# Scan stage of a Mamba block: moving kept output-projection pieces away from the softplus and gate blocks, and adding state pairs by DMA in eight more steps

## The chip, the cores and the metric

The kernel runs on one core of one Trainium2 chip. The metric is the time of one execution on the device, in microseconds (us). The core has four engines that compute, each with its own queue, worked off strictly in order: TensorE (PE: matmuls), VectorE (DVE), ScalarE (ACT: activation functions) and GpSimd (POOL). SyncE (SP) only issues DMA transfers. Engines wait for each other through semaphores.

## The reference, cut to what matters

The whole model is two layers, each a graph or state-space block and a mixture of experts, on 4096 tokens of width 256. The change touches only the state-space (Mamba) block of layer 0:

```
h = relu(adj @ layernorm(x) @ gcn_w + gcn_b);  h = layernorm(h) * ln_g + ln_b
xc, z = split(h @ w_in)                       # 512 channels each
u = silu(causal_conv4(xc) + conv_b)
dt, B, C = split(u @ w_xp);  dt = softplus(dt @ w_dt + b_dt)
for each token:  state = exp(dt * A) * state + dt * B * u     # 512 channels x 16 states
                 ys = sum over the 16 states of state * C
y = (ys + u * D_skip) * silu(z)
x1 = x + y @ w_out
```

`x1` is then layer-normalised and goes to the first mixture of experts.

## The kernel before

Tokens are worked in NC = 8 chunks of CW = 512. The 512 channels are MB = 4 blocks of 128 partitions. The scan stage is a loop over `n`, `c, i = divmod(n, STEPS)`: chunk c, and STEPS = 32 steps i in a chunk. One step works on one channel block (`m`) and two of the 16 states: `half, g, mi` come from i, so i = 0 to 15 are blocks 0 and 1 (alternating), i = 16 to 31 blocks 2 and 3; g is the pair of states.

The order of the work on TensorE, VectorE, ScalarE and GpSimd is the order in which the Python code issues it (`tc.manual_schedule`). SyncE is not in that list: the order of its DMA issues is chosen by the framework. In one turn of the loop, for step n, the code issues:

- GpSimd: `nxt.inputs` (L1138), the product du x bb for step n+1 into `db` (two buffers); and for mi = 0 SyncE loads bb and cb, rows of B and C spread over all partitions (L1134, 512 KB each, two buffers). Then `steps[n-1].pair()` (L1175): in a paired step a DMA issued by GpSimd adds the second state's half of `hc` to the first.
- VectorE: two scans (L1161), each 128 x 512, which need `da`; after each, ScalarE's `nxt.decay` (L1154) writes one of the next step's two `da` tiles, exp(dt x A), into PSUM. Then pieces of the next chunk's preparation on VectorE (`Front.EARLY`), in the last chunk also pieces of the norm (`NORMS`: L965, a pow on GpSimd L968, L974).
- `cur.product`: ScalarE copies the last state (L1167), VectorE multiplies by cb into `hc` (L1171; six buffers).
- `gate` (L1197) for a block that is complete: VectorE multiplies psy by silu(z).
- `total` (L1183, L1188): TensorE adds `hc` to psy of its channel block (`ps_y`, two banks) by products with the identity, one for a paired step and two for an unpaired one; the first of a block also brings u x D_skip (`dD`), and needs the bank that a gate sets free. A paired step's total comes four turns later, an unpaired one's two turns later.
- A piece of the next chunk's preparation, `Front.PLAN`, or, for i < 8, of this chunk's (keys 32 + i): "xz" are matmuls (L787), "in" copies of ScalarE out of PSUM (L794, L800), "silu 2" (keys 39, so i = 7) an activation on 128 x 2048 (L811). Keys 25 to 28 are softplus: "abs", "exp", "plus", "log" on ScalarE (L850 to L863); "soft" 0 to 3 at i = 28 to 31 are eight products on VectorE (L869 to L877).
- `Tail.step(tails)`: one piece of the output projection (below).
- In the last chunk, norm pieces (`NPIECES`, from i = 8: load of x1, normalise L985, turn L998, logits L1010, keep L1016).
- Pieces of the adjacency product two chunks ahead (not in the last two chunks).

Output projections. In chunks 0 to 5 the finished y is kept in DRAM (`keep_gated`), and its projection by w_out is put off. From step (6,8) the kept projections are worked as `Tail`s, half a chunk each, twelve in a row, t0 to t11 here; those of chunk 6 follow from (7,5). A Tail has three pieces, `product(0)`, `product(1)` and `put`; those of chunks 0 to 2 have an empty piece ahead of `put`. `product` (L929 four products, L933 adds the row of x by an identity product) writes the PSUM tile `ps_out`, of which there is one. `put` (L938) has ScalarE copy it to `xr` with row sums and SyncE store it (L943). The squares of a Tail (L948, L952, ScalarE) are left in `Tail.rest` and issued at the start of the next `Tail.step`. When a Tail starts, the following one's loads (`fetch`: x rows into `xr`, L916, two buffers; kept y, L921, three buffers) are issued.

```
while Tail.rest:
    Tail.rest.pop()()
if tails:
    tails[0].todo.pop(0)()
    if len(tails) > 1 and tails[1].xr is None:
        tails[1].fetch()
```

Before the change `Tail.step` is called once in every turn, so that t4 starts at (6,24), t5 at (6,28), t6 at (7,0), t7 at (7,3), t8 at (7,6) and t9 at (7,9). Steps are paired in chunks 0 to 6, and unpaired in chunk 7.

Of the kernel before, what the change touches and what calls it, by code (L numbers as in the profile page):

```python
# [30 lines left out]
def kernel(ctx: ExitStack, tc: tile.TileContext, out: bass.AP, **a):  # L31
# [5 lines left out]
    NC = N // CW  # L37
# [125 lines left out]
    class Dispatch:  # L163
# [4 lines left out]
        def __init__(self, pool, E, name, batches, c0=0):  # L168

            self.E, self.pool, self.name, self.T, self.c0 = E, pool, name, batches, c0  # L170
            self.t0 = [sum(batches[:b]) for b in range(len(batches))]
            self.NT = NT = sum(batches)
            self.K = 2 * NT * P // TR + E - 1
            self.wv = pool.tile([P, NT, 2], F32, name=f"{name}_wv")
            self.hi = pool.tile([P, 2 * NT], F32, name=f"{name}_hi")
            self.lo = None
            self.row = {}
            self.xd = dram.tile([NT * P, D], F32, name=f"{name}_xd")

            self.S = 1 << (NT // TPC - 1).bit_length()  # L180
            self.ys = dram.tile([2 * self.S * CW + self.K * TR, D], F32, name=f"{name}_ys")
            self.count = pool.tile([P, 1, E], F32, name=f"{name}_count")
            self.start()
            self.sent = []

            self.oh = []
            for T in sorted(set(batches), reverse=True):
                n = batches.count(T)
                t = pool.tile([P, n, 2 * T + 1, E], BF16, name=f"{name}_oh{T}")
                nc.gpsimd.memset(t[:, :, :1, :], 0.0)  # L190
                self.oh += [t[:, b] for b in range(n)]

            self.rev = pool.tile([P, max(batches), E], F32, name=f"{name}_rev")
            nc.vector.tensor_scalar(
                self.rev, iota[:, :E].unsqueeze(1).to_broadcast([P, max(batches), E]),
                -1.0, float(E), ALU.mult, ALU.add,
            )

            self.group = pool.tile([P, NT, 2], BF16, name=f"{name}_group")
            for i in range(2):  # L200
                nc.vector.tensor_scalar(
                    self.group[:, :, i], iota[:, :NT], float(i * self.S * TPC), None, ALU.add
                )
# [385 lines left out]
    with ExitStack() as s1:  # L589
# [56 lines left out]
        STEPS = H * 2 * GS  # L646
# [12 lines left out]
        def propagation(c):  # L659


            halves = psts[c] = []
            for r0 in range(c * CW, c * CW + CW, HW):
                pt = ps_pt.tile([P, DB, HW], F32, name="pt", tag="pt")
                for j4 in range(NT // 4):
                    at = ats.pop(0) if ats else adjacency(r0, j4)
                    for jj in range(4):
                        j = 4 * j4 + jj
                        for k in range(DB):

                            nc.tensor.matmul(  # L671
                                pt[:, k, :], xl[:, j, k * P:(k + 1) * P], at[:, jj, :],
                                start=(j == 0 and k == 0), stop=(j == NT - 1 and k == DB - 1),
                            )
                        yield
                pts = w1p.tile([P, DB, HW], F32, name="pts", bufs=2)
                nc.scalar.copy(pts, pt)
                halves.append(pts)
                yield True
# [203 lines left out]
        def keep_gated(c):  # L883

            yd = dram.tile([P, MB, CW], F32, name=f"yd{c}")
            nc.sync.dma_start(yd, fronts[c].us)
            return yd
# [130 lines left out]


        SLOW = 3  # L1020
        NORMS, NPIECES = {}, {}
        for i, c0, c1 in ((1, 0, 3), (13, 3, 5), (19, 5, 6), (25, 6, 7)):
            NORMS[i] = lambda s0=c0 * TPC, n=(c1 - c0) * TPC: Norm.root(s0, n)
# [90 lines left out]
        class Step:  # L1114
# [3 lines left out]
            def __init__(self, c, i):  # L1118
                self.c, self.i = c, i
                self.half, r = divmod(i, 2 * GS)  # L1120
                self.g, self.mi = divmod(r, 2)
                self.m = 2 * self.half + self.mi
                self.f = fronts[c]


                self.paired = c < NC - 1

            def inputs(self, prev):

# [69 lines left out]
        with tc.manual_schedule(engines={  # L1199
# [13 lines left out]
            for _ in range(2 * NT + 2 - sum(FILLED.values())):  # L1213
                i = min(range(STEPS), key=lambda i: pe[i] - PE_RATIO * dve[i])
# [4 lines left out]
            def advance(k=1, wait=False):  # L1219


                while k > 0:
                    k -= 1
                    if next(prop, None) and wait:
                        break
                return k
# [47 lines left out]
            steps, tails, kept, gated, summed, owed = [], [], {}, [], 0, 0  # L1274
            for n in range(NC * STEPS):
                c, i = divmod(n, STEPS)
                if n == 0:
                    cur = Step(0, 0)
                    cur.inputs(None)
                    das = [cur.decay(0), cur.decay(1)]  # L1280
                steps.append(cur)
                if i == 5 and c > 0:
                    if c < NC - 1:
                        kept[c - 1] = keep_gated(c - 1)
                    else:
                        tails.extend(Tail(c - 1, hh) for hh in range(2))
                if i == 8 and c == NC - 2:
                    tails.extend(
                        Tail(k, hh, kept[k], k < SLOW) for k in range(c) for hh in range(2)
                    )  # L1290
                if i == 8:
                    fr = Front(c + 1) if c + 1 < NC else None
                    prop = propagation(c + 2) if c + 2 < NC else iter(())
                if i == STEPS - 1 and fr is not None:
                    fr.at(i, Front.EARLY)
                nxt = Step(*divmod(n + 1, STEPS)) if n + 1 < NC * STEPS else None
                if nxt is not None:
                    nxt.inputs(cur)
                if n > 0:
                    steps[n - 1].pair()  # L1300
                old, das = das, []
                for j in range(2):
                    cur.scan(j, old[j])
                    if nxt is not None:
                        das.append(nxt.decay(j))
                if 7 < i < STEPS - 1 and fr is not None:
                    fr.at(i, Front.EARLY)
                if c == NC - 1 and i in NORMS:
                    NORMS[i]()
                cur.product()  # L1310
                for k in gated:
                    steps[k].gate()
                gated = []
                while summed < n - 1 and (summed < n - 3 or not steps[summed].paired):
                    steps[summed].total()
                    gated.append(summed)
                    summed += 1
                if i < 8:
                    fronts[c].at(STEPS + i)
                elif fr is not None:  # L1320
                    fr.at(i)
                Tail.step(tails)
                if c == NC - 1:
                    for piece in NPIECES.get(i, ()):
                        piece()
                    if i == 22:
                        last = Last()
                        last.first(1)
                    elif i == 24:
                        last.fetch()  # L1330
                    elif i == 25:
                        last.first(0)
                    elif i in (27, 28):
                        last.residual(i - 27)
                owed = advance(pieces[i] + owed, True)
                if i == 7:
                    while owed:
                        owed = advance(owed, True)
                cur = nxt
# [455 lines left out]
```

## Time and profile before

| | us |
|---|---|
| median of 3 runs | 2412.82 (2411.54 to 2413.08) |
| the profiled execution | 2412.49 |
| its span in the profile | 2410.7 |
| TensorE busy in the span | 2239.3 (93%) |
| VectorE busy | 1648.1 (68%) |
| ScalarE busy | 1194.8 (50%) |
| GpSimd busy | 1144.8 (47%) |
| last scan of the scan stage ends | 1245.5 |

In the lines of the profile that follow, a line of the order of time has: start, length (us), engine, line of the kernel, operation, output<-inputs with partitions x elements, count, and in brackets the time that the engine stood idle before it and what ended that. A line of the list of waits has: who waited and for whom, total us, times, longest. A line of the table of stretches has: the stretch and its length, then busy us (and instructions) of PE, PEld (weight loads), DVE, ACT and POOL, then TensorE's granted clock, the DMA engines' busy share and GB/s.

### The profile page before, as it was taken

The page shows a single profiled execution, that of the slowest core. Times are in us where ns is not written, and L with a number is a line of the kernel's source. Part 1 is how long each engine was busy: PE and PEld are TensorE (multiplying, and loading weights), DVE is VectorE, ACT ScalarE, POOL GpSimd, SP SyncE. Part 2 cuts the span into 40 slices and gives each one's busy share as a digit, 9 for nine tenths or more (in the row PEclk, how much of TensorE's full clock was granted, in tenths as well). Part 3 has the DMA queues.
Part 4 walks back from the last instruction along what each step waited for, and adds up shares of the span by engine and source line. Part 5 has one row for each costly group of instructions (what it writes and reads, how often), then busy time and mean ns, then how long its engine had stood idle before and what let it go on. Part 6 is the DMA issues. An engine that isn't in the chain of part 4 may idle for free. (4 is left out here: it accounts for less than half of the span.)

```text
span 2410.7 us, 28097 instructions
## 1 busy us (share of the span) xinstructions
PE 2239.3 (93%) x9018; PEld 1624.2 (67%) x9018; DVE 1648.1 (68%) x2455; ACT 1194.8 (50%) x2050; POOL 1144.8 (47%) x828
## 2 busy tenths in 40 slices
PE   8999999999999999896997999799999999999985
PEld 7665665656465665553666888667888888877774
DVE  2069999999999999998986411291666667742233
ACT  4255666574655666574753322145555555532321
POOL 1057777777877787775644555310000000045652
PEclk9999999999999999998997999999999999999998
DMA  7279999999999999996848877551444444456786
GB/s 237 83 228 227 241 275 238 274 243 268 247 260 258 238 274 238 271 269 174 270 136 266 295 231 228 162 166 53 143 146 148 146 145 146 148 170 209 230 274 235
DMA packets 293071, 511.58 MB, mean 212 GB/s; under 512 B 25376, under 2 KB 159648, under 8 KB 292016
## 3 DMA queue, kind: packets, MB, share of 16 engines
q1 hardware_dynamic: 246640, 412.64, 54.5%
q0 software_dynamic: 46272, 97.03, 18.7%
q8 instruction: 75, 1.23, 0.2%
q14 instruction: 84, 0.69, 0.1%
HBM read 406.03 MB, written 44.83 MB: 187 GB/s over the span
## 5 line engine op out<-in xcount | busy, mean ns | idle before, releaser
L1138 POOL TENSOR_TENSOR db<-du,bb 128x1024 f32<-128x1024 f32 x256 | 607.1, 2372 | 329.5 <-DVE hc L1171 83.1
L1161 DVE TENSOR_TENSOR_SCAN db<-da,state,db 128x512 f32<-128x512 f32 x512 | 627.2, 1266 | 31.5 <-ACT da L1154 29.3
L671 PE MATMUL pt<-at,gn 128*128 128x256 f32 x2048 | 479.4, 387 | 14.9 <-ACT gn L87 9.2
L671 PEld LDWEIGHTS pt<-at,gn 128*128 128x128 f32 x2048 | 397.1, 195 | 135.7 <-issue 63.1
L1154 ACT ACTIVATE da<-dt,negA 128x512 f32<-128x512 f32 x512 | 346.4, 688 | 249.5 <-DVE db L1161 238.7
L1516 PE MATMUL pf<-gn,f 128*128 128x256 f32 x2048 | 452.0, 380 | 0.0
L1516 PEld LDWEIGHTS pf<-gn,f 128*128 128x128 f32 x2048 | 386.6, 190 | 57.2 <-issue 6.4
L1171 DVE TENSOR_TENSOR hc<-db,cb 128x1024 f32<-128x1024 f32 x256 | 328.0, 1281 | 18.2 <-issue 0.4
L1188 PE MATMUL psy<-hc,ident 128*128 128x512 f32 x576 | 301.6, 618 | 4.6 <-DMA hc<-hc 3.7
L81 POOL TENSOR_TENSOR ln_rs<-ln_rs,mhalf 128x4 f32<-128x4 f32 (+1 forms) x25 | 33.4, 1335 | 507.6 <-DVE ln_rs L80 507.1
L508 DVE TENSOR_TENSOR yk<-ps_y,bk 128x512 f32<-128x512 f32 x73 | 50.4, 691 | 308.9 <-PE ps_y L503 232.2
L1505 ACT ACTIVATE f<-f 128x1024 f32<-128x1024 f32 x128 | 134.6, 1057 | 198.7 <-DVE f L1504 128.2
L518 PE MATMUL ps_h<-xkT,wk 128*128 128x256 f32 x864 | 213.6, 388 | 14.7 <-DVE xkT L543 6.9
L503 PE MATMUL ps_y<-wk,hk 128*128 128x256 f32 x864 | 213.3, 382 | 9.2 <-ACT hk L522 6.6
L1175 POOL DMA_DIRECT2D hc<-hc x224 | 195.0, 870 | 0.2
L518 PEld LDWEIGHTS ps_h<-xkT,wk 128*128 128x128 f32 x864 | 159.1, 192 | 50.6 <-ACT hk L522 11.3
L1504 DVE TENSOR_SCALAR f<-at 128x1024 f32<-128x1024 f32 x128 | 88.1, 688 | 148.0 <-PE pf L1516 134.4
L503 PEld LDWEIGHTS ps_y<-wk,hk 128*128 128x128 f32 x864 | 161.9, 191 | 32.7 <-ACT hk L522 8.4
L1188 PEld LDWEIGHTS psy<-hc,ident 128*128 128x128 f32 x576 | 109.3, 196 | 90.2 <-issue 64.0
L1511 DVE SCALAR_TENSOR_TENSOR cnt<-at,cnt 128x1024 bf16<-128x1024 f32 x120 | 145.9, 1216 | 15.9 <-DMA at<-in_adjT_dram 12.3
L1506 ACT ACTIVATE f<-f 128x1024 f32<-128x1024 f32 x128 | 134.5, 1055 | 3.4
L787 PE MATMUL ps_xz<-hT,w_in 128*128 128x512 f32 x256 | 116.3, 597 | 15.2 <-ACT hT L771 8.8
(321 smaller groups left out, 2513.6 us busy)
## 6 DMA issues: line engine op xcount, KB each, us to landing
at<-in_adjT_dram SPq DMA_DIRECT2D x256, 512.0 KB
bb<-bcd SPq DMA_DIRECT2D x128, 512.0 KB
cb<-bcd SPq DMA_DIRECT2D x128, 512.0 KB
hc<-hc POOLq DMA_DIRECT2D x224, 256.0 KB
wk<-in_L_ffn_W_dram SPq DMA_DIRECT2D x70, 512.0 KB
wk<-in_L_ffn_expert_w_dram SPq DMA_DIRECT2D x114, 256.0 KB
yg<-d_ys SPq DMA_DIRECT2D x14, 512.0 KB
yd<-us SPq DMA_DIRECT2D x6, 1024.0 KB
```

The lines of the kernel that those rows point to most:

```text
L503: nc.tensor.matmul(ps[:, j, :], hT[:, m, j * P:(j + 1) * P], w[:, m, :], start=(m == 0), stop=(m == kb_out - 1),)
L518: nc.tensor.matmul(ps[:, j, :], w[:, d, m * P:(m + 1) * P], xT[:, d, :], start=(d == 0), stop=(d == DB - 1),)
L671: nc.tensor.matmul(pt[:, k, :], xl[:, j, k * P:(k + 1) * P], at[:, jj, :], start=(j == 0 and k == 0), stop=(j == NT - 1 and k == DB - 1),)
L1138: nc.gpsimd.tensor_tensor(self.db, self.f.du[self.half][:, self.mi:self.mi + 1, :].to_broadcast([P, 2, CW]), self.bb, ALU.mult,)
L1154: nc.scalar.activation(da, self.f.dt[self.half][:, self.mi, :], AF.Exp, scale=negA[:, self.m, n:n + 1])
L1161: nc.vector.tensor_tensor_scan(self.db[:, j, :], da, self.db[:, j, :], state[:, self.m, n:n + 1], ALU.mult, ALU.add,)
L1171: nc.vector.tensor_tensor(self.hc, self.db, self.cb, ALU.mult)
L1175: nc.gpsimd.dma_start(self.hc[:, 0, :], self.hc[:, 1, :], accum_op=ALU.add)
L1188: nc.tensor.matmul(f.psy[m], ident, self.hc[:, j, :], start=False, stop=(self.g == GS - 1 and j == last),)
L1505: nc.scalar.activation(f, f, AF.Square)
L1511: nc.vector.scalar_tensor_tensor(cnt, at, 0.0, cnt, ALU.is_gt, ALU.add)
L1516: nc.tensor.matmul(pf[:, t, :], f[:, jj, t * P:(t + 1) * P], gn[:, j, :], start=(j == 0 and t % 2 == 0), stop=(j == NT - 1 and t % 2 == 1),)
```

## The change

A table says how many pieces `Tail.step` works in a turn, where it is not one: none at (6,25), (6,26) and (6,28), two each at (6,29) to (6,31); in the last chunk two each at i = 0, 1, 2, 8 and 9 and none at i = 3 to 7. The number of pieces up to the end of (6,31) (24), and up to the end of (7,9), is the same as before. A turn with two pieces issues the squares of a finished Tail ahead of its next piece, in the same turn if the first of its pieces was a `put`. The second part sets `paired` in the first eight steps of the last chunk too, so that their states are added by a DMA, their totals need one product instead of two, and come four turns later instead of two.

```diff
         SLOW = 3
+
+        TAILS = {(NC - 2, i): 0 for i in (25, 26, 28)}
+        TAILS.update({(NC - 2, i): 2 for i in range(29, STEPS)})
+        TAILS.update({(NC - 1, i): 0 if 2 < i < 8 else 2 for i in range(10)})
         NORMS, NPIECES = {}, {}
@@
-                self.paired = c < NC - 1
+                self.paired = c < NC - 1 or i < 8
@@
-                Tail.step(tails)
+                for _ in range(TAILS.get((c, i), 1)):
+                    Tail.step(tails)
```

## The prediction

> **What bounds the kernel now.** I read in this order: the page's busy shares (VectorE is at nine tenths or more through the scan stage), the list of waits between 990 and 1240 us, then the instructions in order of time of VectorE, ScalarE, TensorE and GpSimd there. A step (c,i) is step i of chunk c. Steps are found on VectorE: two scans (L1161) and one product (L1171) each; the gates (L1197) and the norm pieces (L965, L974) say which step it is. An undisturbed step takes 3.68 us from scan to scan.
>
> The list of waits has the loss:
> ```profile
> DVE db L1161 <- ACT da L1154: 17.4, 8, 7.8
> PEld ps_out L929 <- ACT xr L938: 14.2, 3, 10.6
> ```
> VectorE waited eight times for the decay `da`, 17.4 us. Its order of time shows where two thirds of that lie (what stands in brackets is idle time):
> ```profile
> 1129.57 2.45 DVE L1161 TENSOR_TENSOR_SCAN db<-da,state,db 128x512 f32<-128x512 f32 x2
> 1132.11 1.22 DVE L1171 TENSOR_TENSOR hc<-db,cb 128x1024 f32<-128x1024 f32 x1
> 1141.16 2.46 DVE L1161 TENSOR_TENSOR_SCAN db<-da,state,db 128x512 f32<-128x512 f32 x2 [7.83 <-ACT da L1154]
> 1143.73 1.55 DVE L1171 TENSOR_TENSOR hc<-db,cb 128x1024 f32<-128x1024 f32 x1
> 1147.43 2.46 DVE L1161 TENSOR_TENSOR_SCAN db<-da,state,db 128x512 f32<-128x512 f32 x2 [2.15 <-ACT da L1154]
> 1149.98 1.60 DVE L1171 TENSOR_TENSOR hc<-db,cb 128x1024 f32<-128x1024 f32 x1
> 1153.37 2.46 DVE L1161 TENSOR_TENSOR_SCAN db<-da,state,db 128x512 f32<-128x512 f32 x2 [1.79 <-ACT da L1154]
> ```
> These are (7,6) to (7,9): 7.83 + 2.15 + 1.79 = 11.77 us. ScalarE says what held `da`:
> ```profile
> 1139.64 0.39 ACT L938 ACTIVATE xr<-ps_out 128x256 f32<-128x256 f32 x1 [5.45 <-PE ps_out L933]
> ...
> 1140.37 1.30 ACT L1154 ACTIVATE da<-dt,negA 128x512 f32<-128x512 f32 x2
> ```
> The `put` of a tail stood in front of `da`, waiting for TensorE. TensorE's order says why that was late:
> ```profile
> 1113.44 1.10 PE L1188 MATMUL psy<-hc,ident 128*128 128x512 f32 x2 [1.45 <-DMA hc<-hc]
> 1121.86 2.07 PE L1183 MATMUL psy<-us,dD 128*128 128x512 f32 x2 [7.32 <-DVE us L1197]
> 1123.73 3.62 PE L1188 MATMUL psy<-hc,ident 128*128 128x512 f32 x4
> ...
> 1129.98 3.60 PE L787 MATMUL ps_xz<-hT,w_in 128*128 128x512 f32 x8
> 1133.41 1.89 PE L929 MATMUL ps_out<-w_out,at 128*128 128x256 f32 x8
> ```
> It stood still 7.32 us for the gate of (6,30), which frees the bank of chunk 7's first total; then it had all of (7,3) to (7,9) to do at once. The table of stretches shows it busy 41.60 of 41.60 us from 1121.9 to 1163.5. Afterwards it stays nearly as full as VectorE:
> ```profile
> 1163.50:1247.00 83.50, 80.82 (x352) 55.52 (x351) 81.44 (x88) 57.18 (x149) 51.33 (x23) 0.94 0.74 238
> ```
> The first two numbers after the length are TensorE's (80.82) and the third VectorE's (81.44). So a gain in the stalls is kept only as far as TensorE gets ahead too; that is the crux.
>
> **What the Trainium skill says.** "ScalarE: Activation LUTs", What ACT_TABLE_LOAD costs, gives some 1283 ns for a load plus a drain: the trace has 1.28 us at silu (1148.07), so each of softplus and silu brings two loads. "TensorE: Matmul & The Clock Gate", What's actually happening: after an idle window the array runs at half clock until it has been busy for one. The trace agrees: after 9.78 us of idleness the eight matmuls at 1104.29 took 3.24 us to the next, against 1.72 (1133.41 to 1135.14). "SBUF — State Buffer", SBUF: two separate sides: VectorE operations with two SBUF inputs and GpSimd operations lock one port pair. The trace agrees: the small L974 at 1114.17 takes 2.22 us, until GpSimd's product of 1114.02 to 1116.35 is over.
>
> **Unit prices, from start to start.** A float32 matmul is two instructions. Total of one `hc` block: 0.86 us (L1188 x2), so 0.86 paired, 1.72 unpaired; the dD product 0.86. One tail product: 1.72 + 0.43 = 2.16 (1133.41 to 1135.57). xz pair 3.43. turn 0.87, logits 1.71. On ScalarE: `put` 0.73, squares 1.37, da pair 1.3, state copy 0.18, xz copy 0.58. GpSimd: product 2.35, pair DMA 0.87.
>
> **The change, part by part.**
> Chunk 6, i 24 to 31. Eight pieces before and after (24, 27, two each at 29, 30, 31; chunks 0 to 2 have four-piece tails, one piece empty). VectorE's stall of 2.36 before (6,24) comes earlier and stays. That of 1.68 before (6,28) comes from the dt activations and exp; before the change (6,25) held only TensorE work behind dt and (6,26) the empty piece, so clearing them frees nothing: 0. `put` and squares leave (6,27) and (6,28) for (6,29) to (6,31), where VectorE is held by softplus' four products (steps of 5.9 us) and ScalarE idles up to 5.04 us: 0. If that cover failed, 2.1 us.
> (7,0) to (7,2), two pieces each: squares, two products; then put, squares, product; then product and put. ScalarE's busiest is (7,1): 1.3 + 0.18 + 0.73 + 1.37 = 3.6 us in 3.68. TensorE: put at (6,31) done 1104.1, cold product to 1107.9, second to 1110.1; put in (7,1) 1110.9 to 1111.7, squares to 1113.1; product to 1113.8, total, product to 1116.8; put in (7,2) to 1117.6; da for (7,4) to 1118.9, needed at 1121.9. 3 us to spare: 0. The x-row load asked for at 1108.6 (L916) must land by 1113.8; one load shown took from 1001.05 to 1007.72. As late as that, 1115.3, it uses 1.5 of the 3 us.
> Pairs in (7,0) to (7,7). Removed: 8 x 0.86 = 6.9 us of TensorE. Added: eight pair DMAs on GpSimd, behind the next product and ahead of whatever is queued there; 2.35 + 0.87 = 3.22 a step, inside 3.68, as in chunks 0 to 6. Their transfers, 8 x 256 KB, lie where DMA is 0.53 busy: 0. The one queued behind is the pow of NORMS at (7,1), 1110.79: 0.87 later, so L974 waits for a product that starts later. Bounds: -2.1 us (L974 gets the port first) to +0.87; I take +0.8, as here, at 1171 and at 1195 the product went first.
> Order of the totals. (7,0)'s total moves from (7,3) to (7,4), so xz 4 and 5 (3.43 us) run ahead of the wait for the gate, from 1117.7; and totals 7, 8, 9 all fall at (7,11), as 6,31 and 0 and 1 did at (7,3).
> (7,3) to (7,7) without pieces. Two products (4.32 us) less on TensorE, and one put and one squares less on ScalarE. Nothing of TensorE's is then in front of da except the z copies, ready in time. VectorE: (7,3) at 1118.2, (7,7) at 1134.1, (7,8) at 1137.8. At (7,7) silu remains: 1.28 + 1.91 + 1.28 behind the state copy of 1136.7, so da for (7,9) ends 1142.1 and (7,9) starts 1142.15: stall 0.7 (0.87 at the same place of chunk 5, at 863.52). Before 1153.37: **11.2 us earlier**.
> (7,8) and (7,9), two pieces each. ScalarE: squares 1142.9 to 1144.3, da to 1145.5, state, put to 1146.4, squares to 1147.8, da to 1149.1, needed 1149.9: 0. TensorE, idle since about 1141, waits for that put: product 1146.45 to 1150.1 (cold, 1.5 of it), total 1151.0, product 1153.15, three totals 4.3 to 1157.45, turn 1158.3, total 1160.0, product 1162.2, logits. Before, that product ended at 1168.28 and the logits began at 1169.92 after an idle 1.48, with a cold total of 3.28 behind. Next tail product ends: before 1177.39, after 1162.2 + 1.7 + 1.7 + 2.16 = 1167.8: **9.6 us earlier**. VectorE meanwhile stalls 0.9 at (7,15), since the copy of the logits stands before da on ScalarE: 10.3 ahead.
> From there the queues hold the same work as before, TensorE 80.8 us of it, and the end of the stage (L1063, 1255.97) is TensorE's: 9.6 us earlier. The later stages are moved as a block. Sum against the profiled execution: 2412.49 - 9.6 = 2402.9 (its span is 2410.7, 1.8 around it). It stands 0.3 below the median of 2412.82, so I forecast 2403.
>
> **The rivals.**
> A, more: TensorE's idle 1.19 us near 1231 and the half clock after it (L1188 3.41 instead of 1.72, L1010 and L1056 some 1.5 more) vanish, because it is never again ahead, or the clock is not cold at 1146. 9.6 + 1.2 + 3.2 = 14: 2398.5. Against: ScalarE's wait there may only shrink.
> B, same side but small: x-row loads. The load for the product at (7,9) can only be asked after the squares at (7,8), 1144.3; before it had three steps' notice. With the 6.7 us of 1001 and a wait in SyncE's queue of up to 7.5 (longest of L916) it lands between 1151 and 1158.5 instead of 1149.7: 1.4 to 8.9 us of the 9.6 lost: 2404.5 to 2412. For it: one 5.0 us wait of TensorE on this load at (6,9). Against: DMA is half idle here.
> C, slower: SyncE's queue. Its order isn't written by hand, and two stores and one load of the doubled tails stand close at (7,1) and (7,2). If each waits its longest (L943 8.6, L916 7.5, L943 8.6: 24.7) ahead of the load of bb for (7,4), whose lead is 1117.65 - 1107.04 = 10.6, VectorE stands 14.1 us: 2402.9 + 14.1 = 2417, more if cb waits too. It decides from a hold of 20.2 us. Against: each of the three is ready within 4 us by the walk above.
> That the pieces or pairs don't move is excluded: the tables and the flag are read each step.
>
> **How the numbers follow.** Forecast 0.66 (2400 to 2406), A 0.14, B 0.13 at its worse half, C 0.07. A measurement tells some 0.2% (4.8 us) from no change; under 2408 lie the forecast and A: faster 0.80. B gives the same, with a little of C: 0.14. C: slower 0.06. The range, 2397 to 2411, takes A and most of B.
>
> **What would show it.** VectorE: no 7.83 us wait at (7,7), about 0.7 at (7,9), (7,9) some 11 us earlier. GpSimd: L1175 232 times instead of 224. TensorE: L1188 560 instead of 576, an idle stretch of about 5 us before the product at (7,9), three totals at (7,11). L974 some 0.8 later. Wrong if VectorE waits on GpSimd's product for bb, or TensorE on `xr` at (7,9).

## The result and the profile after

| | before | after |
|---|---|---|
| median, us | 2413.22 (17 runs, 2406.98 to 2420.88) | 2406.68 (17 runs, 2400.65 to 2412.11) |
| profiled execution, us | 2412.49 | 2407.69 |
| its span, us | 2410.7 | 2405.8 |

The ratio after to before is 0.9965, with a 95% interval from 0.9953 to 0.9976. That is 8.4 us less (5.8 to 11.3), 0.35%. The forecast was 9.6 us less.

Lines of the scan stage stand 4 higher in the changed kernel (L1161 is L1165, L1171 is L1175, L1063 is L1067); those below the stage's loop stand 5 higher. The two profiles already differ by 0.68 us at (7,6), and did so before the first edited step. So times in the stage are compared from the start of (7,6)'s product: 1132.11 before, 1131.43 after.

The list of waits of the changed kernel, 990 to 1240 us (who waited and for whom, total, times, longest):
```profile
PEld ps_out L929 <- ACT xr L938: 20.1, 4, 9.0
...
DVE db L1165 <- ACT da L1158: 7.8, 8, 2.2
```
VectorE's wait for `da` fell from 17.4 us to 7.8, and the longest from 7.8 to 2.2. TensorE's wait for the `put` grew from 14.2 to 20.1: TensorE is now early. VectorE's order of time in the changed kernel:
```profile
1113.47 2.23 DVE L974 TENSOR_TENSOR x_shift<-x_mean,x_dev 128x12 f32<-128x12 f32 x1
...
1132.58 2.45 DVE L1165 TENSOR_TENSOR_SCAN db<-da,state,db 128x512 f32<-128x512 f32 x2
...
1136.26 2.45 DVE L1165 TENSOR_TENSOR_SCAN db<-da,state,db 128x512 f32<-128x512 f32 x2
...
1140.71 2.46 DVE L1165 TENSOR_TENSOR_SCAN db<-da,state,db 128x512 f32<-128x512 f32 x2 [0.68 <-ACT da L1158]
...
1166.81 2.46 DVE L1165 TENSOR_TENSOR_SCAN db<-da,state,db 128x512 f32<-128x512 f32 x2 [2.21 <-ACT da L1158]
```
(7,7) and (7,8) follow with no wait, 3.68 us apart. At (7,9) 0.68 us are left, behind silu's two table loads. At (7,15) there is a wait of 2.21 us, new in this order, and ScalarE's order says for what:
```profile
1163.97 0.19 ACT L1016 COPY lgs<-ps_lg 128x32 f32<-128x32 f32 x1 [3.62 <-PE ps_lg L1010]
1164.06 2.07 ACT L985 ACTIVATE xn<-xn,x_shift,x_dev 128x256 f32<-128x256 f32 x4
1166.03 1.29 ACT L1158 ACTIVATE da<-dt,negA 128x512 f32<-128x512 f32 x2
```
The copy of the logits waits for TensorE, and `da` stands behind it and the normalising activation (L985). TensorE's order of time:
```profile
1118.02 3.60 PE L787 MATMUL ps_xz<-hT,w_in 128*128 128x512 f32 x8
...
1125.40 1.21 PE L1187 MATMUL psy<-us,dD 128*128 128x512 f32 x2 [2.07 <-DVE us L1201]
...
1144.79 3.78 PE L929 MATMUL ps_out<-w_out,at 128*128 128x256 f32 x8 [4.23 <-ACT xr L938]
1148.83 1.22 PE L933 MATMUL ps_out<-xr,ident 128*128 128x256 f32 x2 [0.25 <-DMA xr<-in_x_dram]
...
1153.05 4.46 PE L1192 MATMUL psy<-hc,ident 128*128 128x512 f32 x10
...
1167.32 0.59 PE L933 MATMUL ps_out<-xr,ident 128*128 128x256 f32 x2
```
The xz product now runs where TensorE stood still for the gate of (6,30). The idle time of 7.32 us there is gone; what is left is one of 2.07 us, for the next gate. At (7,9) TensorE waits 4.23 us for a `put` and then works its eight products at half clock (3.78 us against 1.89). The table of stretches (columns as before; TensorE is the first number after the length, its clock and the DMA share stand behind the counts) shows the price in transfers too. The first line is of the kernel before, the others are of the change:
```profile
1121.90:1163.50 41.60, 41.60 (x120) 23.88 (x121) 29.28 (x24) 23.62 (x52) 18.09 (x8) 0.93 0.53 174
...
1121.20:1162.80 41.60, 34.83 (x107) 20.50 (x106) 40.05 (x35) 28.43 (x65) 31.36 (x17) 0.88 0.98 280
1162.80:1236.30 73.50, 72.31 (x326) 49.89 (x326) 69.56 (x77) 50.90 (x132) 42.15 (x19) 0.98 0.71 228
```
In the first 41.6 us TensorE has 34.83 us of work instead of 41.60, VectorE works 40.05 instead of 29.28, and DMA is 0.98 busy where it was 0.53. Of this the transfers that GpSimd issues take 0.21. The rest are loads that come sooner because VectorE no longer stops: ten of bb and cb are issued in this stretch, seven before. In the 73.5 us behind, TensorE is nearly full again.

### The profile page after: what moved, and what is told of

Its sections match the earlier page's. It is cut to its first block, busy times and chain, and to the rows that moved or that the text cites. A ratio compares the mean times of both kernels' runs of the same rounds, so it can differ in the third digit from the quotient of the medians.

```text
span 2405.8 us, 28085 instructions
## 1 busy us (share of the span) xinstructions
PE 2234.1 (93%) x9002; PEld 1624.5 (68%) x9002; DVE 1648.1 (69%) x2455; ACT 1194.8 (50%) x2050; POOL 1151.7 (48%) x836
## 5 line engine op out<-in xcount | busy, mean ns | idle before, releaser
L1165 DVE TENSOR_TENSOR_SCAN db<-da,state,db 128x512 f32<-128x512 f32 x512 | 627.3, 1266 | 22.3 <-ACT da L1158 20.0
L1175 DVE TENSOR_TENSOR hc<-db,cb 128x1024 f32<-128x1024 f32 x256 | 328.8, 1284 | 18.4 <-PE psy L1192 0.6
L1192 PE MATMUL psy<-hc,ident 128*128 128x512 f32 x560 | 291.5, 614 | 1.8 <-DVE db L1165 0.9
L508 DVE TENSOR_TENSOR yk<-ps_y,bk 128x512 f32<-128x512 f32 x73 | 50.4, 691 | 312.9 <-PE ps_y L503 228.4
L1510 ACT ACTIVATE f<-f 128x1024 f32<-128x1024 f32 x128 | 134.6, 1057 | 202.0 <-DVE f L1509 130.1
L503 PE MATMUL ps_y<-wk,hk 128*128 128x256 f32 x864 | 213.9, 383 | 9.8 <-issue 6.2
L1179 POOL DMA_DIRECT2D hc<-hc x232 | 202.0, 871 | 0.2
L1509 DVE TENSOR_SCALAR f<-at 128x1024 f32<-128x1024 f32 x128 | 87.9, 687 | 149.0 <-PE pf L1521 133.2
L503 PEld LDWEIGHTS ps_y<-wk,hk 128*128 128x128 f32 x864 | 162.3, 192 | 33.6 <-issue 8.0
```

The lines of the kernel that those rows point to most:

```text
L503: nc.tensor.matmul(ps[:, j, :], hT[:, m, j * P:(j + 1) * P], w[:, m, :], start=(m == 0), stop=(m == kb_out - 1),)
L1165: nc.vector.tensor_tensor_scan(self.db[:, j, :], da, self.db[:, j, :], state[:, self.m, n:n + 1], ALU.mult, ALU.add,)
L1175: nc.vector.tensor_tensor(self.hc, self.db, self.cb, ALU.mult)
L1179: nc.gpsimd.dma_start(self.hc[:, 0, :], self.hc[:, 1, :], accum_op=ALU.add)
L1192: nc.tensor.matmul(f.psy[m], ident, self.hc[:, j, :], start=False, stop=(self.g == GS - 1 and j == last),)
L1510: nc.scalar.activation(f, f, AF.Square)
```

## The experiments

Three sets of four kernels were run (e1 to e4, e5 to e8, e9 to e12), each on one chip and beside its own runs of the kernel before. **My theory**: with the stalls gone, TensorE holds the stage's end, so that the end moves only as far as TensorE is ahead; the two parts then partly stand in for each other. **Rivals**: VectorE's own pace holds the end and the parts add up; or the transfers of the pairs set a limit. A second question was why the end of the profiled span moved only 4.9 us.

The stage is compared in this table. Lead is how much earlier VectorE's product of a step starts than in the second profile of the kernel before (e5), counted from (7,6). "Block" is the first product of the last sixteen (L1063 before, L1067 after), the stage's last work on TensorE; its distance from (7,6) is 118.24 us in e5. The ratio is that of the times to the kernel before, on the same chip.

| kernel | stalls at (7,7), (7,8), (7,9) | lead at (7,9) | lead at (7,31) | lead of the block | ratio (95%) |
|---|---|---|---|---|---|
| before (first profile) | 7.83, 2.15, 1.79 | -0.3 | -0.3 | -2.0 | |
| the change (first profile) | 0, 0, 0.68 | 11.7 | 8.7 | 8.6 | 0.9965 (0.9953-0.9976) |
| e6, again | 0, 0, 0.68 | 11.7 | 9.9 | 9.9 | 0.9959 (0.9949-0.9969) |
| e12, again | 0, 0, 0.69 | 11.7 | 10.0 | 9.9 | 0.9971 (0.9959-0.9982) |
| e1, table alone | 0.34, 2.75, 1.80 | 6.6 | 8.1 | 8.0 | 0.9954 (0.9941-0.9967) |
| e10, table alone | 1.62, 2.75, 1.80 | 5.3 | 6.8 | 5.0 | 0.9965 (0.9953-0.9977) |
| e2, pairs alone | 0, 0, 0.83 | 11.6 | 9.6 | 8.0 | 0.9966 (0.9952-0.9979) |
| e11, pairs alone | 0, 0, 0.83 | 11.6 | 9.6 | 7.9 | 0.9976 (0.9967-0.9984) |
| e7, table of chunk 6 alone | 7.44, 2.15, 1.80 | 0.1 | 0.1 | 0.1 | 1.0002 (0.9990-1.0014) |
| e3, pairs to i = 27, no table | 0, 0, 0.82 | 11.6 | 2.2 | -4.6 | 1.0026 (1.0017-1.0034) |
| e4, both, pairs to i = 27 | 0, 0, 0.68 | 11.7 | 2.5 | -4.5 | 1.0010 (1.0000-1.0019) |
| e8, both, four more pairs | 0, 0, 0.68 | 11.7 | 4.9 | -0.4 | 1.0003 (0.9989-1.0017) |
| e9, both, table smoothed | 0, 0, 1.24 | 11.2 | 12.1 | 12.0 | 0.9959 (0.9945-0.9972) |

The traces allow one more comparison, and it speaks for the theory against its first rival. TensorE's lead, read at the second group of logits (L1010), is 9.95 us in e12, 8.16 in e1, 9.63 in e2 and 12.07 in e9, and at the next four groups it is the same within 0.1. VectorE's lead moves to it: from 11.7 at (7,9) down to 10.0 at (7,31) in e12, from 6.6 up to 8.1 in e1, from 11.2 up to 12.1 in e9. The two agree within 0.1 us in every kernel of the table but e3, e4 and e8, which are treated below. So it is TensorE's lead that VectorE ends with; the copies of the logits on ScalarE, which stand ahead of `da`, pass it on.

The lead of the block can be smaller than VectorE's at (7,31) for another reason. In e2 it is 1.7 us smaller; TensorE stood idle 1.37 us for ScalarE's `xnT` just before, and then its order has
```profile
1234.25 7.09 PE L1190 MATMUL psy<-hc,ident 128*128 128x512 f32 x12
```
where the same twelve take 5.40 us in e12. The 1.7 us that e10, e11 and the first profile of before lack are slow products too. So the column for (7,31) is the better one for comparing the two parts.

**e1 and e10: the table alone.** From the changed kernel:
```diff
-                self.paired = c < NC - 1 or i < 8
+                self.paired = c < NC - 1
```


> Only the first part of the change: pieces of the output projections placed as in the change, chunk 7 unpaired throughout. My theory (TensorE's backlog from (7,3) on is what holds the decays): the two products less leave TensorE with totals and xz still in one block behind the gate of (6,30), so VectorE still stalls at (7,7) to (7,9), some 1.3, 3.1 and 2.1 us instead of 7.83, 2.15 and 1.79; TensorE's block of the last products (L1067 in the kernel after) begins 6 to 7.5 us earlier than before. The rival that the placing of the pieces alone makes the gain expects the stalls gone but for 0.7 and the block 10.6 us earlier, as with both parts. Time of the whole: 3 to 7 us below the kernel before.

> The table alone, without pairs, a second time, beside the whole change on the same chip. If the two parts are substitutes for each other, because TensorE holds the stage's end once the stalls are gone, its ratio to before lies within 0.001 of the whole change's. If the parts add, it lies 0.0015 or more above it.

VectorE's order of time in e1:
```profile
1128.75 2.46 DVE L1165 TENSOR_TENSOR_SCAN db<-da,state,db 128x512 f32<-128x512 f32 x2 [0.34 <-ACT da L1158]
...
1135.62 2.46 DVE L1165 TENSOR_TENSOR_SCAN db<-da,state,db 128x512 f32<-128x512 f32 x2 [2.75 <-ACT da L1158]
...
1141.55 2.46 DVE L1165 TENSOR_TENSOR_SCAN db<-da,state,db 128x512 f32<-128x512 f32 x2 [1.80 <-ACT da L1158]
```
Moving the pieces takes away the long stall but leaves the two at (7,8) and (7,9). At (7,8) ScalarE's copies of z wait 3.25 and 1.13 us for xz, which TensorE works behind unpaired totals; at (7,9) silu with its two table loads stands ahead of `da`. That is 5.3 to 6.6 us of lead. The stalls are a little shorter than expected at (7,8) and (7,9), and at (7,7) the two runs of this one kernel differ by 1.3 us. Later VectorE gains 1.5 us more, 0.9 of it because two waits for `da` of 0.28 and 0.61 us near 1200 and 1213 us, which e5 has, do not come here. In time the table alone saved more than the 3 to 7 us expected: by the ratios some 11 us in e1 and 8.4 in e10.

**e2 and e11: the pairs alone.** From the changed kernel:
```diff
-        TAILS = {(NC - 2, i): 0 for i in (25, 26, 28)}
-        TAILS.update({(NC - 2, i): 2 for i in range(29, STEPS)})
-        TAILS.update({(NC - 1, i): 0 if 2 < i < 8 else 2 for i in range(10)})
+        TAILS = {}
```


> Only the second part: pairs added by a DMA in (7,0) to (7,7), one piece in every turn as in the kernel before. My theory: the later total of (7,0) lets xz 4 and 5 run ahead of the gate and eight totals are half as long, so TensorE has no backlog and the stalls at (7,7) and (7,8) vanish although the pieces stand at (7,3) to (7,7); one of about 1 us stays at (7,9) for silu. TensorE's block of the last products begins 10.5 to 12.5 us earlier than before, at least as much as with both parts, because it does not stand idle before the product of (7,9). The rival that the pieces' places make the gain expects stalls of 5 us or more at (7,7) to (7,9) and 3 us or less of gain. Time of the whole: 6 to 10 us below the kernel before.

> The pair DMAs for i < 8 alone, without the table, a second time, beside the whole change on the same chip. Substitutes: ratio within 0.001 of the whole change's. If the parts add: 0.0015 or more above it.

VectorE's order of time in e2, all its waits for `da` from 1120 to 1180:
```profile
1140.31 2.46 DVE L1163 TENSOR_TENSOR_SCAN db<-da,state,db 128x512 f32<-128x512 f32 x2 [0.83 <-ACT da L1156]
...
1165.30 2.46 DVE L1163 TENSOR_TENSOR_SCAN db<-da,state,db 128x512 f32<-128x512 f32 x2 [1.11 <-ACT da L1156]
```
The pairs are enough to have every `put` in time, with the pieces where they were. They do two things, which no run separates: they take 6.9 us from TensorE, and the later total of (7,0) lets xz run ahead of the gate (at 1113.43 in e2). The block came 7.9 to 8.0 us earlier and not 10.5 to 12.5 as expected.

At (7,31) the table alone has a lead of 6.8 to 8.1 us, the pairs alone of 9.6, both together of 8.7 to 10.0. They don't add up: each removes most of the same stall. In time, e10, e11 and e12 ran side by side, and their intervals overlap: no part is shown to be needed beside the other.

**e7: chunk 6 alone.**
```diff
-        TAILS.update({(NC - 1, i): 0 if 2 < i < 8 else 2 for i in range(10)})
@@
-                self.paired = c < NC - 1 or i < 8
+                self.paired = c < NC - 1
```


> Only the part of the table for chunk 6: no piece at (6,25), (6,26) and (6,28), two each at (6,29) to (6,31); chunk 7 as before, no pair DMA. The prediction gave this part 0: stalls of 7.83, 2.15 and 1.79 stay, ratio 0.999 to 1.001. Rival: TensorE's queue at (6,28) to (6,31), where doubled pieces stand ahead of xz and totals, makes (7,0) late: up to 2.1 us, ratio 1.0009; or the freed ScalarE takes part of the 1.68 us stall at (6,28): ratio 0.9993.

The stalls stay, and every lead is 0.1 us: this part alone costs and brings nothing that these runs can tell, as the prediction had it.

**e3 and e4: more pairs.** From the kernel with pairs alone (e3) and from the changed kernel (e4):
```diff
-                self.paired = c < NC - 1 or i < 8
+                self.paired = c < NC - 1 or i < 28
```


> Pairs added by a DMA in 28 steps of the last chunk, pieces as in the kernel before. My theory: in the rest of the last chunk TensorE (80.8 of 83.5 us) is what gives back part of VectorE's lead; 20 more totals of 0.86 us less take it off, VectorE is the bound, and TensorE is not behind at the end: the block of the last products begins 14 to 16 us earlier than before. The rival that VectorE bounds that stretch anyway expects 11 us as with eight pairs; one that GpSimd's queue (2.35 + 0.87 us a step, and the pow of the norms) becomes the bound expects waits of VectorE's scans for db and less than 11 us. For the later stages: if they are bound by loads that go on at their own pace, they give back 60% of any gain, so the whole is 6 us faster; if what is lost there is a matter of chance, the whole is 9 to 13 us faster.

> Both parts of the change, with pairs in 28 steps instead of 8. My theory: the pieces' places bring nothing once TensorE has no backlog: within 1.5 us of the kernel with 28 pairs and the pieces in their old places, both in the start of the last products' block and in time. The rival that placing matters by itself (ScalarE's activations beside softplus and silu) expects 2 us or more below that kernel.

The list of waits of e3, 990 to 1240 us:
```profile
POOL db L1140 <- DMA bb<-bcd: 15.0, 4, 7.2
...
DVE db L1163 <- POOL db L1140: 6.9, 2, 4.6
```
The table of its transfers, 1163 to 1210 us (the last number is the median time from issue to landing):
```profile
hc<-hc POOLq DMA_DIRECT2D x10, 256.0 KB, 7.1
cb<-bcd SPq DMA_DIRECT2D x5, 512.0 KB, 6.5
bb<-bcd SPq DMA_DIRECT2D x5, 512.0 KB, 8.5
```
and its table of stretches:
```profile
1163.00:1210.00 47.00, 37.04 (x170) 27.17 (x169) 39.13 (x34) 28.38 (x76) 30.57 (x21) 0.89 1.03 315
```
The DMA engines have no time left (1.03). The loads of bb take 8.5 us, GpSimd waits 15.0 us for them, VectorE 6.9 us for GpSimd, and TensorE is busy only 37.04 of 47.00 us. The lead of 11.6 us at (7,9) is down to 0.2 at (7,23), and the totals pile up behind the last step: the block is 4.6 us later than before, where 14 to 16 us earlier were expected. The share alone does not tell it. From 1040 to 1080 us of the same run, in chunk 6, where every step is paired, DMA is 1.00 busy and GpSimd does not wait for bb; but there it moves 268 GB/s and not 315, and from 1000 to 1080 us a load of bb takes 7.2 us.

The Trainium skill, "DMA: Bandwidth & Descriptors", Issuing engines are not separate DMA queues, says why GpSimd's own queue does not help: all transfers run on the same 16 engines. The landing times fit that: in e1, without pairs, a load of bb takes 4.6 us from 1122 to 1164.

With the table added (e4) the picture in the stage is the same, and the block is within 0.2 us of e3's. In time e4 is 4.0 us faster by the medians, against the 1.5 us at most that I expected. The stage does not show where that comes from; the two profiles differ by 4.6 us behind the block, as much as those of e1 and e10, one kernel on two chips.

**e8: four more pairs.**
```diff
-                self.paired = c < NC - 1 or i < 8
+                self.paired = c < NC - 1 or i < 8 or i in (12, 16, 20, 24)
```


> The changed kernel with four more paired steps, i = 12, 16, 20 and 24 of the last chunk, which takes 4 x 0.86 = 3.4 us more from TensorE in the stretch where it is nearly full. If what holds the end of the stage is TensorE alone, as I hold, the block of last products starts up to 3.4 us earlier than in the changed kernel, and the ratio to before is lower by up to 0.0014. If four single pair DMAs already hold up bb (as 20 did together, where VectorE waited 4.57 and 2.30 us for the product and the block came 2.5 us later than before), VectorE waits for db one to four times and nothing is won or 2 to 5 us are lost.

The whole gain of the change is lost (1.0003 beside 0.9959 for e6 on the same chip), and neither expected mechanism was seen: VectorE never waits for `db`. It loses its lead mainly in two places: 2.3 us after (7,17), where a gate waits 2.21 us for a total, and 2.7 us after (7,26). At the second its order has
```profile
1218.85 2.39 DVE L130 TENSOR_TENSOR d_oh<-rt_p,rt_red 128x128 bf16<-128x128 f32 x1
```
which takes 0.29 us in the changed kernel. GpSimd's product runs from 1218.76 to 1221.10 beside it, as it did beside L974 in the prediction. TensorE's order shows where it stands still:
```profile
1226.11 3.58 PE L1010 MATMUL ps_lg<-gate_w,xnT 128*128 128x8 f32 x16 [7.60 <-ACT xnT L1006]
```
The copy `xnT` stood on ScalarE behind a `da` that waited for VectorE, and TensorE stood 7.60 us with the totals queued behind the logits. My expectation of up to 3.4 us fell: less work on TensorE brings nothing when a step in the chain from VectorE over ScalarE to TensorE slips. What made it slip is not settled. The four pairs also change the order of the totals, since each comes four turns later and those of the next steps wait behind it; no run separates that from the transfers.

**e9: the idle stretch at (7,9) filled.** One piece in each turn from (7,6) on:
```diff
-        TAILS.update({(NC - 1, i): 0 if 2 < i < 8 else 2 for i in range(10)})
+        TAILS.update({(NC - 1, i): 0 if 2 < i else 2 for i in range(6)})
```


> Both parts, but chunk 7's table has no piece only at i = 3 to 5 (against 3 to 7) and one piece in every later turn (against two at 8 and 9). Up to (7,9) the same ten pieces are worked. If the changed kernel's end is held by TensorE, which stood idle 4 us ahead of the product at (7,9) and ran it cold, then here that idle stretch is filled by the Tail of (7,6) to (7,8), the next wait of VectorE at (7,15) (1.0 to 2.2 us) goes, and the block of last products starts 1 to 2.5 us earlier than in the changed kernel on the same chip, ratio 0.0004 to 0.001 lower. If VectorE's own pace held the end, or if the put at (7,8) makes da late again behind silu (up to 1.5 us at (7,9)), nothing is won.

VectorE's order of time in e9, all its waits for `da` from 1120 to 1232:
```profile
1138.23 2.46 DVE L1165 TENSOR_TENSOR_SCAN db<-da,state,db 128x512 f32<-128x512 f32 x2 [1.24 <-ACT da L1158]
...
1198.48 2.46 DVE L1165 TENSOR_TENSOR_SCAN db<-da,state,db 128x512 f32<-128x512 f32 x2 [0.36 <-ACT da L1158]
```
and of TensorE:
```profile
1139.64 3.45 PE L929 MATMUL ps_out<-w_out,at 128*128 128x256 f32 x8 [2.28 <-ACT xr L938]
```
The `put` at (7,8) does make `da` late (1.24 against 0.69 us), but the wait at (7,15) is gone, TensorE stands 2.28 instead of 4.81 us (e12), and the block leads by 12.0 us against 9.9. VectorE gave 0.5 us away at (7,9), and the stage still ended 2.1 us earlier: this experiment shows most directly that TensorE's lead, and not VectorE's at (7,9), sets the end. The ratio, 0.9959 beside 0.9971 for the change on the same chip, points the same way, but the intervals overlap.

**e5, e6 and e12: the two kernels again.**

> The kernel before, profiled a second time. It shows how much of a difference between two profiles is no difference of the kernels. Three numbers are read. The three stalls at (7,7) to (7,9): 7.83, 2.15 and 1.79 us again, within 0.3, if they are set by the queues. The time from the start of the block of last products (L1063 x16) to the end of the span: 1158.3 us in the first profile against 1164.7 after the change. Theory 1 (what is lost after the scan stage comes from the earlier arrival itself, by what the adjacency loads hold up): before's length stays within 2 us of 1158.3 on the same chip as a profile of the changed kernel that is 3 or more longer, and TensorE's wait at the eighth and ninth expert tile stays at 1.5 us. Theory 2 (chance: transfers fall out otherwise in each execution): the two kernels' lengths differ by less than 3 here, or before's wait there is as long as 2.4.

> The changed kernel again, on this chip, to stand beside the other runs of the same call. The scan stage: product of (7,9) 11 to 12.7 us earlier than before's, the block of last products 10 to 11 earlier, both net of what the two profiles differ by at (7,6). Theory 1 (loss after the stage is systematic): ratio 0.9955 to 0.9975, and the time after the block 3 or more us longer than before's. Theory 2 (chance): same ratio interval, but the lengths after the block differ by less than 3.

> The whole change, on this chip: ratio 0.9955 to 0.997. It is what the three others of this call are compared with. Its profile is the third of this kernel: the block of last products 9.0 to 10.6 us earlier than before's, net of the difference at (7,6); the time after the block tells with the others how far the later stages scatter.

The stalls of before repeat within 0.3 us (7.54, 2.14, 1.80), those of the change within 0.01. Three things do not repeat. First, TensorE near the end of the stage. Its order of time in the first profile of before:
```profile
1232.42 2.66 PE L1010 MATMUL ps_lg<-gate_w,xnT 128*128 128x8 f32 x16 [1.19 <-ACT xnT L1006]
1234.94 2.05 PE L1056 MATMUL ps_out<-xr,ident 128*128 128x256 f32 x4
1236.79 3.62 PE L1188 MATMUL psy<-hc,ident 128*128 128x512 f32 x4
```
and in the second:
```profile
1230.89 1.95 PE L1010 MATMUL ps_lg<-gate_w,xnT 128*128 128x8 f32 x16 [1.20 <-ACT xnT L1006]
1232.69 1.11 PE L1056 MATMUL ps_out<-xr,ident 128*128 128x256 f32 x4
1233.64 1.88 PE L1188 MATMUL psy<-hc,ident 128*128 128x512 f32 x4
```
Half clock followed the same idle 1.2 us once and not the other time: the granted clock is 0.50 from 1236 to 1240 us in the first profile and 1.00 in the second. It made up 1.7 of the 2.0 us by which the block of the first profile is late. So the 10.6 us that the first two profiles show for the block are 8.6 to 9.9 against e5.

Second, the wait at (7,15): 2.21 us in the first profile of the change, 0.94 in the other two.

Third, the time from the block to the end of the span: before 1158.3 and 1166.8, the change 1164.7, 1164.3 and, in e12 on a third chip, 1151.1. On e5's chip the change is 2.5 us shorter there than before, where the first two profiles have it 6.4 us longer; Theory 1 of the expectation falls in that form.

One loss after the stage does come back each time. The result of the ninth expert tile (the ninth L508 on VectorE) comes 112.7, 113.9 and 114.1 us after the block in the three profiles with before's chunk 7 (before, e5, e7), and 116.4, 116.1 and 116.2 in the three of the change. TensorE's order of time there, in e5:
```profile
1358.77 1.13 PE L518 MATMUL ps_h<-xkT,wk 128*128 128x256 f32 x4 [2.05 <-ACT hk L522]
1359.74 0.59 PE L503 MATMUL ps_y<-wk,hk 128*128 128x256 f32 x2
```
and in e6:
```profile
1350.54 2.08 PE L518 MATMUL ps_h<-xkT,wk 128*128 128x256 f32 x4 [2.81 <-ACT f L1510]
1352.41 1.06 PE L503 MATMUL ps_y<-wk,hk 128*128 128x256 f32 x2
```
The wait is 0.8 us longer and the products behind it run at half clock (2.08 and 1.06 us instead of 1.13 and 0.59). The wait is the smaller part. In e7 it is 3.11 us, but the products take 1.13 us and the tile comes at 114.1. From the start of these products to the next full group of L503 it is 3.76 us in e6 and 2.28 in e5, 1.5 us more. ScalarE's `hk` is queued behind a square of the adjacency (L1510); in e6 its input (L1509, VectorE) waited for a load until 1348.16, while DMA was 0.98 busy from 1330 to 1350. Why this happens in the changed kernel stays open. An earlier block alone is not it: e8's block is as late as before's, and its ninth tile comes at 116.5. Nor is it tied to a part of the change: e1 and e10, one kernel, have 115.6 and 114.2.

Whether this loss reaches the end is not shown. At the 31st tile the change is still 2.3 us or more behind (278.6 to 278.8 us after the block, against 274.9 to 276.3). At the 36th, some 610 us later, it stands at 894.7 to 895.3 and the three profiles with before's chunk 7 at 888.7, 892.2 and 895.8.

## Why the prediction was right, and where it was not

- **The stalls (11.77 us, of which 0.7 stays).** Right: 0, 0 and 0.68 or 0.69 us are left, three times. Silu's activation starts 0.01 us after its table load ends (1136.70 after 1136.69), so the drain that the prediction names beside the load is not seen here, and the sum rightly had none.
- **L974 0.8 us later.** Not so. It starts 17.96 us before (7,6)'s product (before 17.94) and takes 2.23 us (2.22): the pair DMA ahead of the pow cost nothing. So the lead at (7,9) was 11.7 to 12.0 us instead of 11.2.
- **Chunk 6: 0.** Right by e7. **(7,0) to (7,2): 0.** Right: VectorE has no wait there.
- **TensorE at (7,9).** It waited for the `put` and ran cold, as said, but from 1145.5 instead of 1146.45 (1144.79 plus the 0.68 of the profiles). The three totals took 4.46 us (4.3). The next Tail's product ended at 1168.43 with the same 0.68 added (1167.8): 9.0 us earlier than before. In e6 it is 9.9 us earlier than in e5.
- **The stall of 0.9 at (7,15).** Right in kind, and the copy of the logits is what it waits for. 2.21 us in the first profile, 0.94 in two more.
- **Transfers of the pairs: 0.** Right in time, but on a cover thinner than the text let on: 0.53 was measured in a stretch in which VectorE stood still for 11.77 us. Once the eight pairs are in and VectorE runs on, 0.98 of the DMA engines' time is busy. Twenty more pairs turned that into a loss.
- **End of the stage 9.6 us earlier, by TensorE.** 9.9, 9.9 and 8.6 against e5, and the lead is TensorE's. Against the profile that the forecast was made from it is 10.6, because that profile held a half-clock stretch near the end; that 9.6 lies between is in part luck.
- **"The later stages are moved as a block."** This step was stated without a reason, and the profiles do not bear it out. Some 2.3 us (116.2 less 113.9) are lost again at the ninth expert tile, in each profile of the change. Whether the loss lasts to the end is open, and the times cannot tell: by their ratios the three measurements are 8.4, 9.9 and 7.0 us, with intervals some 5 us wide that hold the forecast 9.6 as well as 9.9 less 2.3. The first two profiles end only 4.9 us apart, and two profiles of the kernel before differ by 8.5 us behind the block, in stages that the change doesn't touch.

Rival A (more) did not come: the idle 1.19 us near the end stayed. But e9 shows that 2.1 us more lay in the idle stretch at (7,9), which the prediction saw as a cost and not as something to be filled. Rival B, TensorE waiting for the x rows, was 0.25 us at (7,9) in the first profile of the change and 1.93 with the pairs alone (e2). Rival C did not come with the change. What would have shown it, VectorE standing behind GpSimd for bb, came in e3, which has no doubled pieces, so not for C's reason; it sets in between 12 pairs (e8) and 28. How much of it is full DMA engines and how much SyncE's order was not separated.

## What to carry to other kernels

When a stall ends because an engine gets its work in time, ask which engine is nearly as full in the stretch behind it: here the stage's end moved by that engine's lead, a second remedy for the same stall added little, and filling part of that engine's own idle stretch (e9: 2.5 us) added 2.1 us. Work moved from a matmul to a transfer is free only while DMA has room, and a share of DMA read in a stall (0.53) is not the room that will be there when the stall is gone (0.98 in the change; 0.64 with the table alone, in the same stretch of e1). With 28 pairs a load of bb took 8.5 us. Profile the unchanged kernel twice before a difference of 2 us between two profiles is given a cause.

## What the runs showed of the hardware that was not expected

Half clock follows some short idle times and not others. Near the end of the stage TensorE stands idle 1.19 or 1.20 us ahead of the last but one logits in eleven of the profiles, the same work following. From there to the second L1056 (its line in the kernel before) it takes 4.47 us in four of them (e5, e7, e2, e11), 6.16 or 6.17 in five (the change three times, e1, e9) and 7.43 and 7.78 in e10 and the first profile of before. The granted clock there, named above, was 1.00 in e5 and 0.50 in the first profile of before. At the ninth expert tile 2.81 us of idle time were followed by half speed (e6) and 3.11 us by full speed (e7, 1.13 us for the same four products). The Trainium skill, "TensorE: Matmul & The Clock Gate", What's actually happening, has the clock decided in a free-running window of some 3.4 us after an idle one. That half clock does not come each time fits a free-running window; that 1.2 us of idleness can be enough does not fit. What decides it is not shown.
